# Weighted rows in a tile of their own, a precomputed count carry, and two more groups gathered as inputs, in a graph attention layer

## Chip, cores and metric

One core of a Trainium2 chip. The metric is the device time of one execution in microseconds, the median of several runs. Engines: TensorE (PE, with PEld for its weight loads), VectorE (DVE), ScalarE (ACT), GpSimd (POOL), SyncE (SP, which issues most transfers).

## What is computed

A graph attention layer with a residual: 12,500 nodes of 128 features, 200,000 edges of 64 features sorted by destination, 4 heads of 32.

```python
h = jnp.maximum(_layernorm(x, axis=-1), 0.0)
# h_src = (h @ W_node.T)[src], h_tgt the same for dst, e = edge_attr @ W_edge.T
att = jnp.sum(jnp.concatenate([h_src, h_tgt, e], axis=-1) * a, axis=-1)
att = jnp.where(att > 0, att, 0.2 * att)
m = jnp.maximum(jax.ops.segment_max(att, tgt), 0.0)
ex = jnp.exp(att - m[tgt])
denom = jax.ops.segment_sum(ex, tgt) + (num_edges - deg)[:, None] * jnp.exp(-m)
out = x + jax.ops.segment_sum((ex / denom[tgt])[:, :, None] * h_src, tgt)
```

(The last lines are shortened: segment counts are left out.)

## The kernel before

**Tiling.** The edges are cut into 392 groups of 511, each with one slot more (slot 0) for what is carried over from the group before. A group is J = 4 chunks of 128 edges on the partitions. Four groups are a quad (98 quads); two to four quads are a "super", for which one softmax is made. The destinations of a group lie within a window of WIN = 96 nodes.

**Node and index stage (L288 to L423).** For all nodes: layer norm, ReLU, product with the weights; the rows (ROW = 137 numbers: per head 32 values and a one, a count at R_CNT, four source logits from R_SRC) go to `table` in DRAM. Small index tiles (`slot`, `is_last`, `thru`, `cont`) are made beside it.

**Gathers (L128 to L139).** POOL issues one indirect DMA for each chunk of 128 edges, 16 a quad, into `ga_all`, a ring of QUADS = 8 quads. The first RAW = 4 quads gather rows of the input `x` while the table isn't there yet; they are normed and multiplied by the weights later (`normed`, L743; `converted`, L237). All others gather rows of the table. POOL works its gathers in order, each behind the last reader or writer of the ring's place that it overwrites.

**Logits (L493).** For each group DVE compares window positions with destinations (`at`, L500); PE multiplies that by the target logits (`pw`, L505) and the edge features by their weights (L508) into `lg` in PSUM. `open_logits` (L485) issues the transfers of the quad after next, its gathers included. `add_sources` (L511, called by `flush`) adds the gathered source logits on DVE (L520, L522), giving `U`.

**Softmax of a super (L533).** Transposes of `U` on PE (L548), leaky ReLU (ACT L550 and DVE L553), segmented maxima by scans on DVE (L557, L582, L584), exponentials on ACT, transposes back (`ex_ps`; `xs`; carry factors `facs`).

**Sums (L668).** For each group: DVE multiplies the gathered rows by their weights in place (L687), makes the selection matrix `hot` (L691); PE adds chunks 1 to 3 into `acc` (L696). `complete()` then finishes the group before: DVE writes the carry row (last row of the previous `acc` times a factor) into row 0 of `ga` (L634), ACT copies the count into it (L638), PE adds chunk 0 (L639), ACT copies `acc` to `pt` (L640). After a quad's last group, `divide` (L701) runs at the next `complete()`: six DVE operations, then four output transfers on SP, each with a register load (L457) for its address.

**Order.** The order is written by hand: `together` (L141) takes steps in turn from several generators, and the loop at L793 runs the sums of one quad beside the logits of a later one, with the softmax of a super beside the first sums. Each engine works its own instructions in that order.

Of the kernel before, what the change touches and what calls it, by code (L numbers as in the profile page):

```python
# [8 lines left out]
F32 = mybir.dt.float32  # L9
BF16 = mybir.dt.bfloat16  # L10
# [5 lines left out]
P = 128  # L16
# [19 lines left out]
RAW = 4  # L36
# [10 lines left out]
def kernel(  # L47
# [68 lines left out]
    thru = consts.tile([1, G], F32, name="thru")  # L116
    flag = consts.tile([1, 1], I32, name="flag")
# [4 lines left out]
    assert raw == 4 <= nq  # L122
    g_raw = sum(quads[raw - 1])

    ga_all = consts.tile([P, QUADS, QG, J, ROW], F32, name="ga")
    GA = {}

    def gather(q, rows, width):  # L128
# [3 lines left out]
        for i in range(m):  # L132
# [15 lines left out]
    with tc.manual_schedule():  # L148

        nc.sync.dma_start(srci[:, :g_raw], src_by_edge[:, :g_raw])  # L150
        for q in range(raw):
            gather(q, x, D)
# [64 lines left out]
        def gathered_inputs(q):  # L217
            return GA[q][:, :quads[q][1]].rearrange("p g j r -> p (g j) r")[:, :, 0:D]

        def raw_statistics(pool, q):  # L220
            RAWS[q] = yield from statistics(pool, gathered_inputs(q), quads[q][1] * J)

        def raw_scaled(q):

            rows = gathered_inputs(q)
            yield from scaled(rows, rows, quads[q][1] * J, *RAWS.pop(q))
# [10 lines left out]
        def converted(q, psum, turn_pool, copy):  # L237

            ga = GA[q]
            m = quads[q][1]  # L240
# [27 lines left out]
            nc.scalar.copy(rows[:, :, R_CNT], ones[:, 0:m * J])  # L268
# [19 lines left out]
        with tc.tile_pool(name="node", bufs=2) as node, tc.tile_pool(  # L288
# [10 lines left out]
            def indexed():  # L299
# [27 lines left out]
                yield  # L327

# [109 lines left out]
    with tc.tile_pool(name="work", bufs=2) as work, \  # L438
# [18 lines left out]
        def window(g):  # L457
            return nc.values_load(
                base[0:1, g:g + 1], engines=[mybir.EngineType.SP], min_val=0, max_val=N - 1,
                skip_runtime_bounds_check_because="a destination, which is a node")  # L460

        def fetch_windows(q):
# [3 lines left out]
            at = [window(g0 + i) for i in range(m)]  # L466
# [18 lines left out]
        def open_logits(q):  # L485
# [5 lines left out]
            LG[q] = ps.tile([P, QG, J, PIECES, H], F32, name="lg")  # L491
# [41 lines left out]
        def softmax(s):  # L533
# [11 lines left out]
            u = U.pop(s)  # L545
            t_ps = ps.tile([SBG * H, GE], F32, name="t_ps")
# [39 lines left out]
            ex = turned.tile([SBG * H, GE], F32, name="ex")  # L586
# [20 lines left out]
            nc.scalar.copy(facs[:, :R], fac_ps)  # L607
# [3 lines left out]
            xs = turned.tile([P, J, SBG * H], F32, name="xs", bufs=2)  # L611
            nc.scalar.copy(xs[:, :, 0:R], top_ps)
# [5 lines left out]
        begun = []  # L618
        state = {}

        def complete():

            division = state.pop("division", None)
            if begun:
                complete_group(*begun.pop())
            if division:
                divide(*division)

        def complete_group(q, i, ga, hot, pt, acc, fc):
            g0, m = quads[q]  # L630
            g = g0 + i
            if g:
                before = state["before"]
                nc.vector.tensor_tensor(  # L634
                    ga[0:1, i, 0, 0:H * HW].rearrange("p (h w) -> p h w", w=HW),
                    before[WIN:WIN + 1, 0:H * HW].rearrange("p (h w) -> p h w", w=HW),
                    fc.unsqueeze(2).to_broadcast([1, H, HW]), op=OP.mult)
                nc.scalar.copy(ga[0:1, i, 0, R_CNT:R_CNT + 1], before[WIN:WIN + 1, R_CNT:R_CNT + 1])  # L638
            nc.tensor.matmul(acc, hot[:, i, 0, :], ga[:, i, 0, :], start=False, stop=True)  # L639
            nc.scalar.copy(pt[:, i, :], acc)  # L640
            state["before"] = acc

            part = 1 if q == nq - 1 else 2 if q == nq - 2 else QG
            if (i + 1) % part == 0 or i == m - 1:
# [4 lines left out]
                state["division"] = q, pt, den, lo, i + 1  # L649
# [367 lines left out]
```

## Time and profile before

| what | value |
|---|---|
| runs | 2570.87, 2578.58, 2586.93 us; median 2578.58 us |
| profiled execution | 2600.19 us, span 2598.4 us, mean granted TensorE clock 0.536 |
| gathers | 64 of inputs (3.2 to 83.1 us), 1502 of the table (161.1 to 2473 us) |
| ACT `pt` copy L640 | 392 x 274 ns |
| DVE weighting L687 | 392 x 689 ns |
| DVE selection L691 | 384 x 545 ns |
| ACT source copy L680 | 392 x 216 ns |

In a row of the groups, the first number behind the bar is the busy time of all, the second the mean of one in ns; then comes the idle time of the engine just before them and what ended it. "Issue" is time in which the engine waited for nothing that the profile shows; "remote" is a releaser that the profile can't name. In a timeline each line gives start, duration, engine, source line and tiles, with the idle time before it in brackets. Line numbers are those of the kernel before.

### The profile page before, as it was taken

How to read it: one execution, taken by the hardware profiler on the slowest of the kernel's cores; microseconds unless marked ns; L12 is line 12 of the kernel's file. 1: busy time of each engine (PE TensorE's matmuls, PEld its weight loads, DVE VectorE, ACT ScalarE, POOL GpSimd, SP SyncE). 2: the span in 40 equal slices, each digit the busy share in tenths (PEclk: the TensorE clock that was granted, in tenths of full speed). 3: DMA queues.
4: the chain of work that ended last, by engine and by line, in shares of the span. 5: the costliest groups of instructions: out<-in, count | busy, mean ns of one | idle time of the engine just before them, and what ended most of it. 6: DMA issues, size and time to landing. Idle time of an engine off the chain costs nothing. (4 is left out here: it accounts for less than half of the span.)

```text
span 2598.4 us, 29393 instructions
## 1 busy us (share of the span) xinstructions
PE 1405.4 (54%) x7275; PEld 1256.7 (48%) x7275; DVE 1367.0 (53%) x3291; ACT 421.7 (16%) x1806; POOL 1508.0 (58%) x1609
## 2 busy tenths in 40 slices
PE   2442665555555555556555555655555555545485
PEld 1331655545545445445445544545544554444375
DVE  2441465555555545555554554654554554555486
ACT  1431411111111111111111111111111111111122
POOL 7235256666666666666666666666666666666603
PEclk9975655555555555555555555555555555555555
DMA  4342455544544454554455445454544544434430
GB/s 150 102 126 53 108 136 124 127 116 118 128 123 113 115 142 107 127 125 117 119 124 124 116 119 123 120 125 117 125 115 118 125 121 116 121 97 112 103 92 17
DMA packets 214495, 299.12 MB, mean 115 GB/s; under 512 B 86121, under 2 KB 162153, under 8 KB 204914
## 3 DMA queue, kind: packets, MB, share of 16 engines
q1 hardware_dynamic: 162512, 184.97, 26.6%
q0 software_dynamic: 50112, 109.65, 19.3%
q10 hardware_dynamic: 1698, 2.58, 0.3%
q8 instruction: 61, 1.00, 0.2%
q14 instruction: 112, 0.92, 0.1%
HBM read 270.49 MB, written 26.52 MB: 114 GB/s over the span
## 5 line engine op out<-in xcount | busy, mean ns | idle before, releaser
L137 POOL DMA_INDIRECT ga<-table,srci x1502 | 1426.7, 950 | 963.2 <-issue 406.0
L696 PE MATMUL acc<-ga,hot 128*97 128x137 f32 x2352 | 649.6, 448 | 341.3 <-ACT ga L680 225.1
L696 PEld LDWEIGHTS acc<-ga,hot 128*97 128x97 f32 x2352 | 518.2, 279 | 366.1 <-ACT ga L680 229.2
L634 DVE TENSOR_TENSOR ga<-acc,facs 1x132 f32<-1x132 f32 x391 | 115.9, 296 | 625.9 <-ACT pt L640 502.1
L639 PE MATMUL acc<-ga,hot 128*97 128x137 f32 x784 | 267.4, 444 | 289.0 <-ACT ga L638 215.5
L508 PE MATMUL lg<-wblk,ea 128*128 128x8 f32 x1568 | 410.5, 360 | 0.0
L508 PEld LDWEIGHTS lg<-wblk,ea 128*128 128x128 f32 x1568 | 383.3, 310 | 0.0
L505 PEld LDWEIGHTS <-at 96*128 96x128 bf16 x1568 | 219.7, 167 | 298.7 <-DVE at L500 115.0
L639 PEld LDWEIGHTS acc<-ga,hot 128*97 128x97 f32 x784 | 190.3, 279 | 320.3 <-ACT ga L638 235.8
L640 ACT COPY pt<-acc 97x137 f32<-97x137 f32 x392 | 107.4, 274 | 1431.8 <-remote 850.5
L505 PE MATMUL lg<-pw,at 96*128 96x12 bf16 x1568 | 170.7, 182 | 239.1 <-DVE at L500 101.2
L687 DVE TENSOR_TENSOR ga<-ga,ex_ps 128x528 f32<-128x528 f32 x392 | 270.0, 689 | 8.4 <-remote 8.0
L500 DVE TENSOR_TENSOR at<-const_ps,db 96x512 bf16<-96x512 f32 x392 | 267.1, 683 | 9.0 <-DMA db<-in_dst_dram 3.2
L691 DVE TENSOR_TENSOR hot<-const_ps,slot 128x384 f32<-128x384 f32 x384 | 209.4, 545 | 0.0
L520 DVE TENSOR_REDUCE st<-lg 128x64 f32<-128x192 f32 x98 | 35.0, 358 | 139.1 <-remote 109.7
L638 ACT COPY ga<-acc 1x1 f32<-1x1 f32 x391 | 59.9, 153 | 228.8 <-DVE ga L634 114.1
L375 PE MATMUL row_ps<-wcat,hT 128*128 128x137 f32 x198 | 40.3, 354 | 79.9 <-DVE hT L367 32.0
L600 PE MATMUL ex_ps<-ident,ex 64*128 64x64 f32 (+2 forms) x112 | 18.6, 315 | 115.6 <-ACT ex L589 49.7
L375 PEld LDWEIGHTS row_ps<-wcat,hT 128*128 128x128 f32 x198 | 34.0, 246 | 86.1 <-issue 46.0
L553 DVE TENSOR_TENSOR t_ps<-t_ps,low 64x511 f32<-64x511 f32 (+2 forms) x28 | 19.2, 687 | 104.4 <-issue 60.2
L137 POOL DMA_INDIRECT ga<-in_x_dram,srci x64 | 60.6, 947 | 20.9 <-issue 19.2
L600 PEld LDWEIGHTS ex_ps<-ident,ex 64*128 64x128 f32 (+2 forms) x112 | 13.8, 208 | 118.3 <-ACT ex L589 51.1
(131 smaller groups left out, 1131.1 us busy)
## 6 DMA issues: line engine op xcount, KB each, us to landing
db<-in_dst_dram SPq DMA_DIRECT2D x98, 768.0 KB
ea<-in_edge_t_dram SPq DMA_DIRECT2D x98, 512.0 KB
ga<-table,srci POOLq DMA_INDIRECT x1502
xw<-in_x_dram SPq DMA_DIRECT2D x392, 48.0 KB
out_dram<-res SPq DMA_DIRECT2D x392, 48.0 KB
pw<-side SPq DMA_DIRECT2D x392, 2.2 KB
table<-row SPq DMA_DIRECT2D x9, 616.5 KB
xt<-in_x_dram SPq DMA_DIRECT2D x9, 576.0 KB
```

The lines of the kernel that those rows point to most:

```text
L137: nc.gpsimd.indirect_dma_start(out=ga[:, i, j, 0:width], out_offset=None, in_=rows, in_offset=bass.IndirectOffsetOnAxis(ap=srci[:, g0 + i, ...
L375: nc.tensor.matmul(row_ps[:, t, :ROW], hT[:, t, :], wcat, start=True, stop=True)
L500: nc.vector.tensor_tensor(at[:, i, :], node_ps[0:WIN, g0 + i:g0 + i + 1].to_broadcast([WIN, GE]), db[:, i, :], op=OP.is_equal)
L505: nc.tensor.matmul(lg[:, i, j].rearrange("p k h -> p (k h)"), at[:, i, j * P:(j + 1) * P], sw, start=i + j == 0, stop=False, skip_group_ch ...
L508: nc.tensor.matmul(lg[:, i, 2 * w:2 * w + 2, 0, :], ea[:, i, w, :], wblk, start=False, stop=True, skip_group_check=True)
L634: nc.vector.tensor_tensor(ga[0:1, i, 0, 0:H * HW].rearrange("p (h w) -> p h w", w=HW), before[WIN:WIN + 1, 0:H * HW].rearrange("p (h w) -> ...
L638: nc.scalar.copy(ga[0:1, i, 0, R_CNT:R_CNT + 1], before[WIN:WIN + 1, R_CNT:R_CNT + 1])
L639: nc.tensor.matmul(acc, hot[:, i, 0, :], ga[:, i, 0, :], start=False, stop=True)
L640: nc.scalar.copy(pt[:, i, :], acc)
L687: nc.vector.tensor_tensor(val, val, heads(ex)[:, :, :, g - s0].unsqueeze(3).to_broadcast([P, J, H, HW]), op=OP.mult)
L691: nc.vector.tensor_tensor(hot[:, i, :, 0:WIN], lane_ps.unsqueeze(1).to_broadcast([P, J, WIN]), slot[:, g, :].unsqueeze(2).to_broadcast([P, ...
L696: nc.tensor.matmul(acc, hot[:, i, j, :], ga[:, i, j, :], start=j == 1, stop=False)
```

## The change

- `sums` no longer weights in place: DVE multiplies `ga` into a new tile `gw` (pairs of groups, two buffers), which PE reads. ACT fills count and source columns of `gw` once per two groups, from a constant tile `xs_all` whose ones and source columns the softmax writes.
- The count that is carried over is computed for all groups in the index stage (`came`: four products, a scan) and copied once for each super; the ACT copy L638 goes.
- The copy of `acc` to `pt` (`copied`) is issued one `complete()` later than before, the division one or two later again; three calls of `complete()` end the program.
- The leaky ReLU becomes one DVE operation on `U`, ahead of the transposes. Carry factors are copied by DVE, one row only.
- `lg` has two halves of one PSUM tile; in `all_logits` the first group's logits come before `flush`.
- SP loads four window addresses at once.
- `marks` is called quad by quad at the end, `hot` has two buffers instead of three.
- RAW stays 4, and MORE = 2 groups of quad 4 gather inputs too. They are normed beside `sums` of quad 0 and converted behind quad 3. The two other groups of quad 4 gather from the table.

```diff
@@ -33,7 +33,7 @@
 NODE_T = 9
-RAW = 4
+RAW, MORE = 4, 2
 QUADS = 8
@@ -114,22 +114,26 @@
     thru = consts.tile([1, G], F32, name="thru")
+    came = consts.tile([1, G + 1], F32, name="came")
     flag = consts.tile([1, 1], I32, name="flag")
 ...
     raw = RAW
-    assert raw == 4 <= nq
-    g_raw = sum(quads[raw - 1])
+    assert raw == 4 < nq and MORE < quads[raw][1]
+    g_raw = quads[raw][0] + MORE
+    raws = lambda q: quads[q][1] if q < raw else MORE if q == raw else 0
     ga_all = consts.tile([P, QUADS, QG, J, ROW], F32, name="ga")
-    GA = {}
-    def gather(q, rows, width):
+    GA, GATHERED = {}, set()
+    def gather(q, rows, width, lo, hi):
         g0, m = quads[q]
         ga = GA[q] = ga_all[:, q % QUADS]
-        for i in range(m):
+        for i in range(lo, hi):
             n = -(-min(E - (g0 + i) * NE + 1, GE) // P)
@@ -148,8 +152,9 @@
         nc.sync.dma_start(srci[:, :g_raw], src_by_edge[:, :g_raw])
-        for q in range(raw):
-            gather(q, x, D)
+        GATHERED.update(range(raw))
+        for q in range(raw + 1):
+            gather(q, x, D, 0, raws(q))
@@ -215,15 +220,15 @@
         def gathered_inputs(q):
-            return GA[q][:, :quads[q][1]].rearrange("p g j r -> p (g j) r")[:, :, 0:D]
+            return GA[q][:, :raws(q)].rearrange("p g j r -> p (g j) r")[:, :, 0:D]
         def raw_statistics(pool, q):
-            RAWS[q] = yield from statistics(pool, gathered_inputs(q), quads[q][1] * J)
+            RAWS[q] = yield from statistics(pool, gathered_inputs(q), raws(q) * J)
         def raw_scaled(q):
             rows = gathered_inputs(q)
-            yield from scaled(rows, rows, quads[q][1] * J, *RAWS.pop(q))
+            yield from scaled(rows, rows, raws(q) * J, *RAWS.pop(q))
         def several(n, *steps):
@@ -325,6 +329,15 @@
                 yield
+                ones_b = index.tile([P, 1], BF16, name="ones_b")
+                nc.vector.memset(ones_b, 1.0)
+                own_ps = wide_ps[0][0:1, :]
+                for j in range(J):
+                    nc.tensor.matmul(own_ps, ones_b, is_last[:, :, j], start=j == 0, stop=j == J - 1)
+                nc.vector.memset(came[:, 0:1], 0.0)
+                yield
+                nc.vector.tensor_tensor_scan(came[:, 1:G + 1], thru, own_ps, initial=0.0,
+                                             op0=OP.mult, op1=OP.add)
                 nc.vector.tensor_scalar(slot[0:1, :, 0], cont, -1.0, None, op0=OP.add)
@@ -444,8 +457,14 @@
         share_ps = const_ps[0:WIN, WIN + G:].rearrange("p (g h) -> p g h", h=H)
+        lg_all = ps.tile([P, 2, QG, J, PIECES, H], F32, name="lg")
         nc.vector.tensor_copy(lane_ps, lane)
         nc.vector.tensor_copy(node_ps, node_at)
+        xs_all = consts.tile([P, 2, J, 1 + H, SBG], F32, name="xs_all")
+        nc.vector.memset(xs_all[:, :, :, 0, :], 1.0)
         tops = consts.tile([1, H, len(supers) + 1], F32, name="tops")
@@ -454,16 +473,18 @@
             return g0, quads[q0 + m - 1][0] + quads[q0 + m - 1][1] - g0
-        def window(g):
-            return nc.values_load(
-                base[0:1, g:g + 1], engines=[mybir.EngineType.SP], min_val=0, max_val=N - 1,
-                skip_runtime_bounds_check_because="a destination, which is a node")
+        def windows(q, lo=0, hi=QG):
+            g0, m = quads[q]
+            g0, m = g0 + lo, min(hi, m) - lo
+            return nc.values_load_multi_w_load_instructions(
+                base[0:1, g0:g0 + m], engines=[mybir.EngineType.SP], min_val=0, max_val=N - 1,
+                skip_runtime_bounds_check_because="a destination, which is a node")[1]
         def fetch_windows(q):
 ...
             xw = XW[q] = work.tile([WIN, QG, D], F32, name="xw", bufs=8)
-            at = [window(g0 + i) for i in range(m)]
+            at = windows(q)
             for i in range(m):
@@ -473,8 +494,9 @@
             fetch_windows(q)
-            if q not in GA:
-                gather(q, table, ROW)
+            if q not in GATHERED:
+                GATHERED.add(q)
+                gather(q, table, ROW, raws(q), quads[q][1])
         def fetch_rows(s):
@@ -488,7 +510,7 @@
             AT[q] = work.tile([WIN, QG, GE], BF16, name="at")
-            LG[q] = ps.tile([P, QG, J, PIECES, H], F32, name="lg")
+            LG[q] = lg_all[:, q % 2]
         def logits(q, i):
@@ -543,14 +565,14 @@
             u = U.pop(s)
+            nc.vector.scalar_tensor_tensor(u[:, :, :R], u[:, :, :R], SLOPE, u[:, :, :R],
+                                           op0=OP.mult, op1=OP.max)
             t_ps = ps.tile([SBG * H, GE], F32, name="t_ps")
 ...
             low = turned.tile([P, NE], F32, name="low")
-            nc.scalar.mul(low[:R], t_ps[:R, 1:GE], SLOPE)
             yield
             att = t_ps[:R, 1:GE]
-            nc.vector.tensor_tensor(att, att, low[:R], op=OP.max)
             run = turned.tile([SBG * H, GE], F32, name="run")
@@ -604,49 +626,55 @@
             facs = turned.tile([P, SBG * H], F32, name="facs", bufs=2)
-            nc.scalar.copy(facs[:, :R], fac_ps)
+            nc.vector.tensor_copy(facs[WIN:WIN + 1, :R], fac_ps[WIN:WIN + 1, :])
             top_ps = other[:, 512 - J * SBG * H:].rearrange("p (j r) -> p j r", j=J)[:, :, 0:R]
 ...
                 nc.tensor.transpose(top_ps[:, j, :], run[:R, j * P:(j + 1) * P], ident[:R, :R])
-            xs = turned.tile([P, J, SBG * H], F32, name="xs", bufs=2)
-            nc.scalar.copy(xs[:, :, 0:R], top_ps)
+            xs = xs_all[:, s % 2]
+            nc.scalar.copy(xs[:, :, 1:, 0:m], top_ps.rearrange("p j (h g) -> p j h g", h=H))
+            nc.scalar.copy(xs[0:1, 0, 0, 0:m], came[:, g0:g0 + m])
             XS[s] = ex_ps[:, 0:J * SBG * H].rearrange("p (j r) -> p j r", j=J), xs, facs
             yield
-        begun = []
+        begun, divisions = [], []
         state = {}
         def complete():
-            division = state.pop("division", None)
+            due = [d for d in divisions if d[0] >= nq - 2 or d[-1] == 1]
+            divisions[:] = [d[:-1] + (1,) for d in divisions if d not in due]
+            full = state.pop("full", None)
             if begun:
                 complete_group(*begun.pop())
-            if division:
-                divide(*division)
-        def complete_group(q, i, ga, hot, pt, acc, fc):
-            g0, m = quads[q]
-            g = g0 + i
-            if g:
+            if full:
+                copied(*full)
+            for d in due:
+                divide(*d[:-1])
+        def complete_group(q, i, gw, hot, pt, acc, fc):
+            if quads[q][0] + i:
                 before = state["before"]
                 nc.vector.tensor_tensor(
-                    ga[0:1, i, 0, 0:H * HW].rearrange("p (h w) -> p h w", w=HW),
+                    gw[0:1, 0, 0:H * HW].rearrange("p (h w) -> p h w", w=HW),
                     before[WIN:WIN + 1, 0:H * HW].rearrange("p (h w) -> p h w", w=HW),
                     fc.unsqueeze(2).to_broadcast([1, H, HW]), op=OP.mult)
-                nc.scalar.copy(ga[0:1, i, 0, R_CNT:R_CNT + 1], before[WIN:WIN + 1, R_CNT:R_CNT + 1])
-            nc.tensor.matmul(acc, hot[:, i, 0, :], ga[:, i, 0, :], start=False, stop=True)
+            nc.tensor.matmul(acc, hot[:, i, 0, :], gw[:, 0, :], start=False, stop=True)
+            state["before"] = acc
+            state["full"] = q, i, pt, acc
+        def copied(q, i, pt, acc):
             nc.scalar.copy(pt[:, i, :], acc)
-            state["before"] = acc
             part = 1 if q == nq - 1 else 2 if q == nq - 2 else QG
-            if (i + 1) % part == 0 or i == m - 1:
+            if (i + 1) % part == 0 or i == quads[q][1] - 1:
                 lo = i - i % part
 ...
                                      AF.Exp, scale=-1.0)
-                state["division"] = q, pt, den, lo, i + 1
+                divisions.append((q, pt, den, lo, i + 1, 2))
@@ -656,7 +684,7 @@
             g0, m = quads[q]
-            hot = work.tile([P, QG, J, WIN + 1], F32, name="hot", bufs=3)
+            hot = work.tile([P, QG, J, WIN + 1], F32, name="hot")
             nc.scalar.copy(hot[:, :m, :, WIN], is_last[:, g0:g0 + m, :])
@@ -677,15 +705,21 @@
             for i in range(m):
-                nc.scalar.copy(ga[:, i, :, R_SRC:R_SRC + H], heads(xs)[:, :, :, g0 - s0 + i])
-            for i in range(m):
                 g = g0 + i
-                if q == nq - 1 - FREE and i == 1:
-                    for k in range(FREE):
-                        HOT[nq - FREE + k] = marks(nq - FREE + k)
-                val = ga[:, i, :, 0:H * HW].rearrange("p j (h w) -> p j h w", w=HW)
+                if i == 1 and nq > q + 1 >= nq - FREE:
+                    HOT[q + 1] = marks(q + 1)
+                if i % 2 == 0:
+                    gw2 = work.tile([P, 2, J, ROW], F32, name="gw")
+                    n = min(2, m - i)
+                    nc.scalar.copy(
+                        gw2[:, 0:n, :, R_CNT:R_SRC + H],
+                        xs[:, :, :, g - s0:g - s0 + n].rearrange("p j h g -> p g j h"))
+                gw = gw2[:, i % 2]
+                by_head = lambda t: t[:, :, 0:H * HW].rearrange("p j (h w) -> p j h w", w=HW)
                 nc.vector.tensor_tensor(
-                    val, val, heads(ex)[:, :, :, g - s0].unsqueeze(3).to_broadcast([P, J, H, HW]),
+                    by_head(gw), by_head(ga[:, i]),
+                    heads(ex)[:, :, :, g - s0].unsqueeze(3).to_broadcast([P, J, H, HW]),
                     op=OP.mult)
@@ -693,9 +727,9 @@
                 for j in range(1, J):
-                    nc.tensor.matmul(acc, hot[:, i, j, :], ga[:, i, j, :], start=j == 1, stop=False)
+                    nc.tensor.matmul(acc, hot[:, i, j, :], gw[:, j, :], start=j == 1, stop=False)
                 complete()
-                begun.append((q, i, ga, hot, pt, acc, fc[:, :, g - s0]))
+                begun.append((q, i, gw, hot, pt, acc, fc[:, :, g - s0]))
                 yield
@@ -720,13 +754,16 @@
             add.tensor_tensor(res[:, :n, :], res[:, :n, :], xw, op=OP.add)
+            at = windows(q, lo, hi)
             for i in range(n):
-                nc.sync.dma_start(out[bass.ds(window(quads[q][0] + lo + i), WIN), :], res[:, i, :])
+                nc.sync.dma_start(out[bass.ds(at[i], WIN), :], res[:, i, :])
         def all_logits(q):
+            open_logits(q)
+            logits(q, 0)
+            yield
             flush()
-            open_logits(q)
-            for i in range(QG):
+            for i in range(1, QG):
                 logits(q, i)
@@ -803,18 +840,20 @@
                     now, ahead = ahead[:1], ahead[1:]
-                    together(sums(q0 + k), *map(all_logits, now))
+                    together(sums(q0 + k), *map(all_logits, now), *([] if s else [normed(raw)]))
                     if s > 4:
 ...
                     complete()
+                    complete()
                     together(*late(3))
+                    together(*late(raw))
             flush()
             together(sums(nq - 1))
-            complete()
-            complete()
+            for _ in range(3):
+                complete()
             together(check_steps)
```

The parts left out bring `raws(q)` into the conversion, reuse a tile in the check of the input's order, and leave the count column of converted rows unwritten.

More of the change, by code (lines that the diff above doesn't have):

```diff
@@ L239, in converted @@
             ga = GA[q]
-            m = quads[q][1]
+            m = raws(q)
             made = []
@@ L267, in converted @@
                 ones[:, 0:1].unsqueeze(2).to_broadcast([P, m * J, H]))
-            nc.scalar.copy(rows[:, :, R_CNT], ones[:, 0:m * J])
             yield
@@ L585, in softmax @@
                                          initial=0.0, op0=OP.mult, op1=OP.max)
-            ex = turned.tile([SBG * H, GE], F32, name="ex")
+            ex = turned.tile([P, GE], F32, name="ex")
             nc.vector.memset(ex[:R, 0:1], 0.0)
@@ L764, in checked @@
             for k, (g0, n) in enumerate(blocks(G, P)):
-                rows = turned.tile([P, NE + 1], I32, name="rows")
+                rows = turned.tile([P, GE], F32, name="ex").bitcast(I32)
                 nc.scalar.dma_start(rows[:n], dst_rows[g0:g0 + n, 0:NE + 1])
-                yield
                 falls = turned.tile([P, NE], F32, name="low")
@@ L791 @@
                 together(all_logits(q), raw_statistics(raw_pool, 3))
+            assert supers[0] == (0, 2) and supers[1] == (2, 2)
             check_steps = checked()
```

## Prediction

> **What bounds the kernel now.** I read the page's busy shares first, then the slices, the table of windows, the groups by line, and last the timeline of a stretch in mid-run.
>
> ```profile
> PE 1405.4 (54%) x7275; PEld 1256.7 (48%) x7275; DVE 1367.0 (53%) x3291; ACT 421.7 (16%) x1806; POOL 1508.0 (58%) x1609
> L137 POOL DMA_INDIRECT ga<-table,srci x1502 | 1426.7, 950 | 963.2 <-issue 406.0
> L640 ACT COPY pt<-acc 97x137 f32<-97x137 f32 x392 | 107.4, 274 | 1431.8 <-remote 850.5
> L634 DVE TENSOR_TENSOR ga<-acc,facs 1x132 f32<-1x132 f32 x391 | 115.9, 296 | 625.9 <-ACT pt L640 502.1
> ```
>
> No engine is full: 54, 53 and 58%. POOL is nearest: a gather takes 0.95 us and the next starts 0.30 us later (406 us of "issue" over 1,394 gaps), 1.25 us each, 5.0 us a group of four. ACT is nearly idle, yet its `pt` copy waits 850 us for a "remote" releaser (no finished instruction accounts for it), and the carry row on DVE waits behind it for 502 us.
>
> ```profile
> 0.00:83.00 83.00, 15.54 (x55) 11.81 (x55) 14.93 (x77) 12.47 (x30) 61.50 (x72) 1.00 0.41 129
> 83.00:161.00 78.00, 45.02 (x258) 38.59 (x258) 51.44 (x224) 52.79 (x134) 0.06 (x1) 0.89 0.43 146
> 161.00:241.00 80.00, 11.39 (x44) 8.76 (x44) 6.95 (x27) 6.59 (x19) 60.40 (x64) 0.54 0.30 72
> 241.00:295.00 54.00, 36.82 (x236) 34.78 (x237) 32.08 (x95) 28.69 (x81) 0.00 (x0) 0.59 0.35 88
> ```
>
> Columns: window, length, busy us of PE, PEld, DVE, ACT, POOL, then clock, DMA share, GB/s. Where POOL gathers without a pause (0 to 83, 161 to 241) PE is busy 14 to 19% of the time; where POOL rests, 58 to 68%. From 295 to 2473 us there are 1,438 gathers, 359.5 groups, in 2,178 us: 6.06 us a group (5.97 between 1000 and 1500), against 5.0 of POOL and about 3.2 each of PE and DVE (54%, 53% of 6). The timeline shows why:
>
> ```profile
> 1484.94 0.66 PE L639 MATMUL acc<-ga,hot 128*97 128x137 f32 x2
> ...
> 1486.45 0.22 PE L505 MATMUL lg<-pw,at 96*128 96x12 bf16 x2 [0.85 <-issue]
> ...
> 1488.82 0.94 POOL L137 DMA_INDIRECT ga<-table,srci  x1 [0.30 <-issue]
> ...
> 1491.72 0.28 ACT L640 COPY pt<-acc 97x137 f32<-97x137 f32 x1 [8.21 <-remote]
> 1491.95 0.94 POOL L137 DMA_INDIRECT ga<-table,srci  x1 [2.19 <-remote]
> 1492.02 0.30 DVE L634 TENSOR_TENSOR ga<-acc,facs 1x132 f32<-1x132 f32 x1 [4.55 <-ACT pt L640]
> ...
> 1492.96 0.69 DVE L687 TENSOR_TENSOR ga<-ga,ex_ps 128x528 f32<-128x528 f32 x1
> ```
>
> L639 ended at 1485.60, but ACT, which waits for it, started at 1491.72: 1.96 us after POOL's last gather ended (1489.76). POOL itself waits for the same L639, to overwrite that group's rows. So while POOL gathers, the others learn late that PE is done. I counted pauses (a gather with over 1 us of idle before it) from 400 to 2300 us: 137 runs of 8 or 12 gathers mostly (58 and 59; also 19 of 4, one of 16), on average 2.31 groups, with pauses of 2.57 us. PE completions in the first 5 to 5.5 us of a run are seen promptly, later ones nearly all about 2.2 us after it stops. The loop: POOL runs c groups, stops at a row not yet known to be free, all is seen 2.2 us later, everybody works from then until about 5.5 us into the next run. Check: 5.0 + (2.57 − 0.30)/2.31 = 5.98 us a group, as measured.
>
> Here a rule could undo the reading. The Trainium skill (Perfetto Trace Analysis, "Tensor Engine Instruction") says that a PE end is an estimate, not an observation. By the rule the 6 us after L639 could be PE still at work, then shortening the chain behind PE is worth nothing (time unchanged, 2,579 us). The rows decide otherwise: PE, which works in order, started L505 at 1486.45, so L639 was past by then. I use the rows.
>
> **The change, part by part**, against the profiled execution (2,600.19 us, span 2,598.4).
>
> *The ring's release.* DVE now writes weighted rows into `gw`, so POOL's gather waits for DVE's multiply instead of L639; the built program has 370 POOL waits on DVE (11 before), 77 on PE (365 before). In group number, rows are free about three groups earlier, since the multiply of group n+3 is issued about when L639(n) is seen. That offset is won once: about 3 groups go from a 6 us pace into a tail without gathers, where the pace is near 4; I take −7 us. But the multiply of n+3 stands in DVE's order behind the carry row of n+1, which waits for the last matmul of n. So at each stop POOL still needs PE's completion to be seen, and after it DVE's carry row (0.30), often a logits compare or `add_sources` (0.6), and the multiply (0.69): 1.5 to 2 us more. Before, POOL restarted at once at that point, and the multiply came later: after the restart at 1491.95 it ended at 1493.65. Bounds for the pause: 2.57 (multiply already done) to 5.0 (a divide, 2.2 us, lies ahead of it too); taken 4.05.
> *What the longer pause gives back.* The working stretch is pause − 2.2 + 5.5: before 5.87 us for 2.31 groups, 2.54 us a group; after 7.35 us. The cost of a group in it falls: L634 no longer waits on L640 (0.24 us at 1483.02), L638 (153 ns ×391) goes, L553 (687 ns ×28, 0.05 a group): to 2.29. So c = 7.35/2.29 = 3.2, and a group takes 5.0 + (4.05 − 0.30)/3.2 = 6.17 us against 5.98, **+0.19 ×355 = +67 us**. By the ends: a pause of 2.57 with 2.29 gives c 2.56 and 5.89 (−33 us); 5.0 with 2.54 gives c 3.27 and 6.44 (+161 us).
> *ACT and semaphores.* L638 and four 216 ns copies a quad become one copy per two groups; `pt` copies lag one group. ACT is 16% busy, so its 60 us lie beside all else; only the hops counted above stand on the path. PE updates fall from 2256 to 1416. If late delivery depended on their number it would ease; in the 80 us run one got through in about 10 us (L263 at 175.30 and 185.11), however few there were, so 0; else the onset moves from 5.5 to at most 7.5 us: c = 4.1, 5.92 us, −23 us.
> *SP.* 785 register loads become 201. SP issues for two quads ahead; four `pw` issues stretched over 12.6 us (at 182.97) and no group waited for them (L500 waits 3.2 us in all, for `db`). 0; if that cover were gone, 0.7 us a quad, 70 us at most.
> *Leaky-relu before the transposes.* L550 (588 ns, waits 159.5 us for remote) and L553 go; one DVE operation 128x256 comes, 0.44 us by a line through 128x64 (269) and 64x511 (677): on DVE −7 us in all, already in 2.29. The skill (SBUF, "Who interferes with whom") says that a DVE instruction with two SBUF inputs contends with a GpSimd instruction that reads SBUF; the new one has two. By the rule 28 × 0.44 = up to 12 us are lost by gathers. The nearest row is L722, two SBUF inputs: at 1485.09 it took 0.71 us beside a gather of 0.94 us, both as usual. I take 0.
> *Double logits, deferred divide, spread marks.* The first logits go ahead of the flush, the divide behind a later carry row: an order change on DVE with the same instruction count. Where the divide falls in a pause it costs its 2.2 us, in one of four groups; that is in the pause's bound.
> *Two more raw groups.* Eight gathers move ahead of the table: the first run ends at 93 instead of 83, so the backlog and the table come about 10 us later (171), and the second run is 56 instead of 64 gathers, 10 us shorter. Net 0. If the node stage does use the 10 us it is −4. The conversion costs eight transposes, eight products, four copies of 0.39, two of 0.69, and norms beside `sums(0)`, on a path where the engines wait for each other: +7 us (0 to +12). The `came` row is some five small operations in the index stage, beside POOL's pause, +1.
>
> Sum: +67 − 7 + 7 + 1 = +68: 2,668 for a profiled execution. That of before is 21.6 us above the median of the runs, so about **2,647 us**.
>
> **Rivals.**
> - *About the same.* Four groups in each cycle: 5.0 + 3.75/4 = 5.94 us; −15 us with nothing else, 2,565 to 2,600. For it: 12-gather runs are already half of all. Against: DVE is full in the working stretches (1492.0 to 1497), so 1.84 us a group is needed.
> - *Faster.* POOL's row is freed by DVE, whose signals are prompt, and the lead of three groups covers the late PE signal. For it: DVE and ACT signals show no delay. If the multiply does not have to wait for PE (two `gw` pairs would have to suffice for c groups), pauses shrink to below 1.6 us per 3 groups: 5.43, −195 us, 2,385. A half success, 5.7, gives 2,480. Against: `gw` itself is freed by PE. It decides once the pause divided by c falls below 0.9 us.
> - *Much slower.* Divide or the softmax's chain stands ahead of the multiply in most pauses: 6.44 and beyond, 2,740 to 2,790. For it: 2.2 us every quad and some 12 us of DVE every 16 groups. Against: DVE takes part of it while PE's signals are held back.
> - *Nothing.* Ring and hops cost nothing because pauses are set by SP or DMA (share 0.5): 2,579. Against: POOL's waits end at L639 of the same group.
>
> **How the numbers follow.** Forecast (1 to 4.5% slower) 0.45, much slower 0.20, same or nothing 0.15, faster 0.20. Within 1% is what the measurement cannot tell from no change (the three runs lie 0.6% apart). So faster 0.20, same 0.15, slower 0.65. The forecast's own range is 2,605 to 2,695. For 8 in 10 I take in half of each flank: 2,520 to 2,770.
>
> **What would show it.** Right: POOL's gathers wait for the multiply; fewer pauses (about 115 instead of 137 in 1,900 us), each 3.7 to 4.5 us, runs of 12 and 16; late PE signals as before; 6.1 to 6.3 us a group in the middle; the second run of gathers still ends near 241. Wrong: pauses under 3 us with runs of 12 or more, or PE's signals prompt in long runs (then faster); pauses at 5 us and more, with the divide in them (then much slower).

## The result and the profile after

The changed kernel takes 2,832.31 us (median of four, 2,828.62 to 2,835.44) against 2,575.08 us, **1.099 times** the time before (95% interval 1.0949 to 1.1032). The forecast was slower, 2,647 us, with 2,770 us as the upper end: right in sign, with 2.7% where 9.9% came. The profiled execution took 2,833.38 us, its span is 2,831.5 us. The kernel before took 2,568 to 2,611 us in some groups of runs, this result's among them, and 2,026 to 2,036 us in others, with the same program, so every ratio is taken against the runs of before beside it.

The busy shares and the groups of the page, changed kernel:

```profile
PE 1427.4 (50%) x7303; PEld 1248.0 (44%) x7303; DVE 1374.0 (49%) x3337; ACT 333.2 (12%) x1205; POOL 1504.5 (53%) x1609
L141 POOL DMA_INDIRECT ga<-table,srci x1494 | 1415.4, 947 | 1176.0 <-DVE gw L720 559.8
L660 DVE TENSOR_TENSOR gw<-acc,facs 1x132 f32<-1x132 f32 x391 | 115.8, 296 | 926.6 <-remote 817.0
```

Hardly any engine has more work: POOL 1,504.5 us (1,508.0 before), DVE 1,374 (1,367), PE 1,427 (1,405); ACT has 88 us less. All are idle longer. POOL's idle before gathers grew from 963 to 1,176 us, and its largest part now names DVE's multiply (L720). The carry row (L660) waits for an unnamed releaser for 817 us, as ACT's copy did before for 850 us.

The windows of the same kernel (columns as in the table of windows shown before):

```profile
0.00:83.00 83.00, 15.53 (x55) 11.81 (x55) 14.87 (x78) 13.95 (x33) 61.55 (x72) 1.00 0.40 129
...
171.00:241.00 70.00, 11.94 (x44) 9.46 (x44) 8.22 (x29) 9.83 (x26) 51.20 (x55) 0.53 0.27 73
...
1000.00:1500.00 500.00, 249.83 (x1290) 217.64 (x1290) 241.66 (x551) 41.45 (x174) 281.91 (x297) 0.51 0.44 110
```

The last of these stretches in the kernel before:

```profile
1000.00:1500.00 500.00, 281.98 (x1444) 253.06 (x1444) 268.80 (x607) 66.68 (x329) 317.54 (x335) 0.50 0.50 120
```

In the middle 297 gathers fall into 500 us where 335 did: 6.7 us a group instead of 6.0. The second run of gathers goes from 173.3 to 243.1, some 2 us later than worked out (171 to 241).

Where the 233 us of span went can be read from the start of the multiply of a given group in both traces: group 32 starts 36 us later (532.1 against 496.1); from there to group 360 it takes 2,160.6 us instead of 1,970.0, which is **191 us**; behind it 6.4 us are lost.

The runs and pauses of POOL, counted in the traces as for the prediction (400 to 2300 us, a pause being over 1 us of idle before a gather):

| kernel | pauses | groups a run | mean pause, us | DVE busy in a pause, us | us a group |
|---|---|---|---|---|---|
| before | 137 | 2.31 | 2.57 | 0.48 | 6.00 |
| changed | 77 | 3.74 | 6.31 | 3.33 | 6.62 |

5.0 + (6.31 − 0.30)/3.74 gives 6.61, so the same sum holds with other terms. The same pauses, sorted by what DVE did inside them:

| inside the pause (over 0.3 us of it) | changed: pauses, mean us | before: pauses, mean us |
|---|---|---|
| softmax | 34, 8.33 | 32, 2.72 |
| a division, no softmax | 3, 7.30 | none |
| neither | 40, 4.51 | 105, 2.52 |

So it is the softmax that makes the long pauses of the changed kernel, while before it cost POOL next to nothing. A pause of 8 to 12 us comes at nearly every 64th gather of the changed kernel, once a super of four quads. One of them in the timeline of the changed kernel:

```profile
1479.75 0.95 POOL L141 DMA_INDIRECT ga<-table,srci  x1 [0.31 <-issue]
...
1483.20 0.15 DVE L602 COPY col<-ex_ps 64x1 f32<-64x1 f32 x1 [5.22 <-remote]
1483.45 1.28 DVE L604 TENSOR_TENSOR_SCAN t_ps<-kp,col,t_ps 64x511 f32<-64x511 f32 x1
...
1486.72 0.63 ACT L611 ACTIVATE ex<-ex 64x511 f32<-64x511 f32 x1 [11.46 <-DVE ex L610]
...
1489.15 0.23 DVE L629 COPY facs<-acc 1x64 f32<-1x64 f32 x1 [0.78 <-PE acc L627]
1489.41 0.70 DVE L720 TENSOR_TENSOR gw<-ga,ex_ps 128x528 f32<-128x528 f32 x1
...
1490.38 0.95 POOL L141 DMA_INDIRECT ga<-table,srci  x1 [9.69 <-DVE gw L720]
```

POOL stopped at 1480.70 (1479.75 + 0.95), after 16 gathers. PE's signal was seen 2.5 us later (1483.20). Then the rest of the softmax ran, because the multiply that frees POOL's row uses its exponentials and stands behind it on DVE: POOL rested 9.69 us. Before, the row was freed by L639 of an earlier group, and POOL went on at about 2.2 us while softmaxes and divisions ran beside its next gathers.

### The profile page after: what moved, and what is told of

Same layout as the page of the kernel before. It is cut to its first block, busy times and chain, and to the rows that moved or that the text cites. A ratio compares the mean times of both kernels' runs of the same rounds, so it can differ in the third digit from the quotient of the medians.

```text
span 2831.5 us, 27061 instructions
## 1 busy us (share of the span) xinstructions
PE 1427.4 (50%) x7303; PEld 1248.0 (44%) x7303; DVE 1374.0 (49%) x3337; ACT 333.2 (12%) x1205; POOL 1504.5 (53%) x1609
## 4 chain that ended last, share of the span: by engine, by line
another core or an unknown queue 36%; DVE 33%; PE 15%; issue 6%; DMA 1%; ACT 1%; SPq 0%; DVEq 0%; POOL 0%; POOLq 0%; ACTq 0%
PE acc L730 6%; DVE gw L720 6%; DVE at L522 6%; DVE hot L725 4%; PE lg L530 3%; DVE gw L660 3%; PE acc L664 2%; DVE res L756 2%; DVE res L752 2%; DVE t_ps L604 1%; DVE t_ps L606 1%; PE acc L266 1%; PE acc L627 1%; DVE U L544 1%
## 5 line engine op out<-in xcount | busy, mean ns | idle before, releaser
L730 PE MATMUL acc<-gw,hot 128*97 128x137 f32 x2352 | 642.5, 444 | 67.9 <-DVE hot L725 16.7
L664 PE MATMUL acc<-gw,hot 128*97 128x137 f32 x784 | 267.6, 444 | 667.7 <-DVE gw L660 579.2
L660 DVE TENSOR_TENSOR gw<-acc,facs 1x132 f32<-1x132 f32 x391 | 115.8, 296 | 926.6 <-remote 817.0
L730 PEld LDWEIGHTS acc<-gw,hot 128*97 128x97 f32 x2352 | 514.1, 277 | 99.6 <-issue 55.2
L664 PEld LDWEIGHTS acc<-gw,hot 128*97 128x97 f32 x784 | 185.4, 274 | 707.2 <-DVE gw L660 609.2
L527 PEld LDWEIGHTS <-at 96*128 96x128 bf16 x1568 | 212.6, 165 | 284.3 <-issue 138.4
L720 DVE TENSOR_TENSOR gw<-ga,ex_ps 128x528 f32<-128x528 f32 x392 | 270.7, 690 | 1.3
L141 POOL DMA_INDIRECT ga<-in_x_dram,srci x72 | 68.3, 949 | 23.3 <-issue 21.6
L692 POOL TENSOR_SCALAR hot<-lane,slot 128x96 f32<-128x96 f32 x32 | 17.1, 554 | 105.2 <-ACT hot L688 94.1
L752 DVE TENSOR_TENSOR res<-pt,const_ps 96x512 f32<-96x512 f32 (+2 forms) x102 | 67.5, 662 | 7.1 <-DMA out_dram<-res 3.1
```

The source lines that it names most:

```text
L141: nc.gpsimd.indirect_dma_start(out=ga[:, i, j, 0:width], out_offset=None, in_=rows, in_offset=bass.IndirectOffsetOnAxis(ap=srci[:, g0 + i, ...
L527: nc.tensor.matmul(lg[:, i, j].rearrange("p k h -> p (k h)"), at[:, i, j * P:(j + 1) * P], sw, start=i + j == 0, stop=False, skip_group_ch ...
L660: nc.vector.tensor_tensor(gw[0:1, 0, 0:H * HW].rearrange("p (h w) -> p h w", w=HW), before[WIN:WIN + 1, 0:H * HW].rearrange("p (h w) -> p ...
L664: nc.tensor.matmul(acc, hot[:, i, 0, :], gw[:, 0, :], start=False, stop=True)
L720: nc.vector.tensor_tensor(by_head(gw), by_head(ga[:, i]), heads(ex)[:, :, :, g - s0].unsqueeze(3).to_broadcast([P, J, H, HW]), op=OP.mult)
L730: nc.tensor.matmul(acc, hot[:, i, j, :], gw[:, j, :], start=j == 1, stop=False)
```

## The experiments

**Theory.** PE's signals are seen late while POOL gathers. With the ring freed by DVE's multiply, POOL runs on longer, more is late when it stops, and in the pause it also waits for DVE's chain. **Rivals:** the tile itself (its two buffers, DVE's writes); the order (deferred copies and divisions, logits ahead of the flush); the two raw groups.

Not every run shows PE's signals late. In the changed kernel's trace above 104 of 287 carry rows (400 to 2300 us) start over 1 us after the modelled end of the product that they wait for, with DVE idle; in another trace of the same program, below, none of 338 does (from 400 us on). I call the first kind of run "late" and the second "prompt". The loss is seen in late runs alone, so these decide.

### Rows weighted in place: first, second and third time

```diff
-                    gw2 = work.tile([P, 2, J, ROW], F32, name="gw")
+                    gw2 = ga[:, i:i + 2]
```

> The changed kernel with the rows weighted in place again, so that a gather waits for PE's last matmul as before; everything else of the change stays. Theory (the ring's release behind DVE's multiply makes POOL's runs and pauses long): back near the kernel before, 2,540 to 2,610 us, runs of about 2.3 groups with pauses of about 2.6 us. Rival 'order' (deferred copies and divisions, logits ahead of the flush): stays within 2,780 to 2,850 us. Rival 'raw groups': stays too.

> The changed kernel with rows weighted in place, as in the first experiments. Where the kernel before takes 2,029 us: 2,039 us again. Where it takes about 2,575 us: theory 2,540 to 2,610 us, pauses near 2.6 us; rivals 'order' and 'raw groups' 2,780 to 2,850 us.

> The changed kernel with rows weighted in place, a third time, since the chips so far were of two kinds: on two of them the kernel before takes 2,029 us and PE's signals are prompt, on the others 2,575 to 2,600 us with late signals. With late signals: theory 2,530 to 2,640 us, runs of 2 to 2.7 groups, pauses of 2.4 to 3.2 us; rivals 'order' and 'raw groups' 2,780 to 2,860 us. With prompt signals 2,030 to 2,045 us, as before.

The first two met prompt signals: 2,039.31 us, 1.0047 times before (1.0030 to 1.0064), and 2,038.17, 1.0044 (1.0030 to 1.0058). They tell nothing of the loss. The third met late ones: 2,636.98 against 2,577.76 us, **1.023** (1.0183 to 1.0281; two runs). Its page:

```profile
L141 POOL DMA_INDIRECT ga<-table,srci x1494 | 1415.0, 947 | 1001.0 <-issue 472.9
```

POOL's idle is 1,001 us, where it was 1,176 in the changed kernel and 963 before. The time is as expected; the mean pause of 3.33 us and the runs of 2.87 groups are somewhat longer than expected (up to 3.2 us and 2.7 groups), at 6.08 us a group. The rivals "order" and "raw groups" needed 2,780 us or more: they fall as causes of the bulk.

### The tile kept, the ring freed by PE: twice

```diff
+            nc.tensor.matmul(bank[0:1, 256:320], rows[:, 0:1], rows[:, 0:64], start=True, stop=True)
```

(behind the last matmul of a group; `rows` are the unweighted rows of its first chunk, `bank` the PSUM bank of `acc`. The gathers of the other three chunks stand behind the first one on POOL.)

> The changed kernel, tile and all, with one small product more per group (1 row of 64, from the unweighted rows, result unused), put behind the group's last matmul: POOL's gather then waits for PE again although rows are weighted in a tile of their own. Theory: 2,540 to 2,620 us, pauses near 2.6 us. Rival 'the tile itself' (its two buffers make DVE wait for PE, or DVE's writes are dearer): stays at 2,780 to 2,860 us.

> The changed kernel, tile, deferred copies and all, with the small product from the unweighted rows behind each group's last matmul, so that POOL's gather waits for PE again. So far it met prompt signals only (2,043 us beside 2,029). With late signals: theory (the release of the ring through DVE makes the loss) 2,590 to 2,690 us, near the 2,637 us of in-place weighting; rival 'the tile itself': 2,780 to 2,860 us. With prompt signals 2,035 to 2,050 us.

First prompt: 2,042.81 us, 1.0066 (1.0049 to 1.0083). Then late: 2,639.80 against 2,570.94 us, **1.026** (1.0212 to 1.0313; two runs). The groups of this late run:

```profile
L141 POOL DMA_INDIRECT ga<-table,srci x1494 | 1412.7, 946 | 995.4 <-issue 407.9 <-remote 170.3 <-PE acc L665 127.7
...
L665 PE MATMUL acc<-ga 128*1 128x64 f32 x784 | 143.6, 284 | 0.0
L660 DVE TENSOR_TENSOR gw<-acc,facs 1x132 f32<-1x132 f32 x391 | 115.9, 296 | 631.5 <-remote 388.8 <-PE acc L732 130.8 <-PE acc L665 48.3
```

POOL waits for PE again and its idle is back from 1,176 to 995 us. PE has 144 us of products more, and still the kernel stands at 1.026 times before, where the changed one stood at 1.099. Pauses are 3.03 us, DVE is busy for 0.90 us of them (3.33 in the changed kernel), 6.06 us a group. Softmax falls into 7 of its 120 pauses (34 of 77 in the changed kernel). Tile, deferred copies, order and raw groups are all still there, so freeing the ring by DVE without PE is what costs some 7 of the 10 points. With the in-place run, which undoes it in another way and lands within 0.3 points, this is the decisive experiment.

### The changed kernel as it is, beside before

> The changed kernel as it is, beside the kernel before, because in the first experiments the kernel before itself took 2,029 us, POOL gathered without a pause and no signal of PE was late. Where the kernel before takes about 2,029 us again: theory says no cost of the change, 2,025 to 2,045 us, because its loss needs late signals. Where the kernel before takes about 2,575 us: 2,820 to 2,840 us again. Rival 'the loss is the change's own work or order': 8 to 10% slower in both cases.

2,035.84 us, **1.0022** (1.0011 to 1.0034), prompt, as expected for that case. The windows of this run:

```profile
0.00:83.00 83.00, 52.23 (x275) 43.40 (x276) 60.62 (x283) 55.39 (x139) 61.55 (x72) 0.87 0.71 231
...
1000.00:1500.00 500.00, 332.78 (x1731) 302.53 (x1731) 320.58 (x729) 55.74 (x238) 378.52 (x399) 0.50 0.62 143
```

POOL does the same 61.55 us of gathers in the first 83 us, but PE is busy for 52 us beside them instead of 15.5. In the middle POOL gathers without a pause, 399 in 500 us, 5.0 us a group. A stretch of its timeline:

```profile
1003.49 0.67 PE L664 MATMUL acc<-gw,hot 128*97 128x137 f32 x2
...
1003.91 0.94 POOL L141 DMA_INDIRECT ga<-table,srci  x1 [0.30 <-issue]
...
1004.19 0.30 DVE L660 TENSOR_TENSOR gw<-acc,facs 1x132 f32<-1x132 f32 x1 [0.45 <-PE acc L664]
```

The carry row starts 0.03 us after PE's modelled end, in the middle of a POOL run. Without late signals the change costs 0.2%: its own work and order make no loss of 10% by themselves.

### Without the two raw groups

```diff
-RAW, MORE = 4, 2
+RAW, MORE = 4, 0
```

(and without their norm and conversion)

> The changed kernel without the two raw groups of the fifth quad. Theory: within 15 us of the changed kernel (2,820 to 2,845 us), the pace in the middle the same 6.6 us a group. Rival 'raw groups': under 2,780 us.

2,035.12 us in one run, prompt, beside 2,029.41 of before and 2,035.84 of the changed kernel in the runs above: the raw groups move nothing that one run shows. The expected 2,820 to 2,845 us were for late signals, with which this was not tried.

### The tile alone on the kernel before

```diff
-                val = ga[:, i, :, 0:H * HW].rearrange("p j (h w) -> p j h w", w=HW)
+                if i % 2 == 0:
+                    gw2 = work.tile([P, 2, J, ROW], F32, name="gw")
...
+                gw = gw2[:, i % 2]
```

(and two `hot` buffers instead of three, to make room, with `marks` called quad by quad at the end)

> The kernel before with only the tile of weighted rows added (pairs of groups, two buffers; its source and count columns copied by ACT), and two hot buffers instead of three to make room. Theory: about as slow as the changed kernel, 2,760 to 2,880 us, with runs of 3.5 groups or more and pauses of 5 to 7 us. Rivals 'order' and 'raw groups': near 2,580 us.

> The kernel before with only the tile of weighted rows added, again, for a chip with late signals (on a chip with prompt signals it took 2,037 us beside 2,029). With late signals: theory 2,740 to 2,860 us, 3.3 groups a run or more, pauses over 5 us, since in-place weighting took 7 of the 10 per cent of the change away. Rival 'the tile does harm only together with the deferred copies and divisions': 2,560 to 2,640 us. With prompt signals 2,030 to 2,045 us.

> The kernel before with only the tile of weighted rows added, a third time, still for a chip with late signals, where it hasn't run. With late signals: theory 2,740 to 2,860 us, 3.3 groups a run or more, pauses over 5 us. Rival 'the tile does harm only together with the deferred copies and divisions': 2,560 to 2,640 us. With prompt signals 2,030 to 2,045 us.

> The kernel before with only the tile of weighted rows added, a fourth time: it hasn't run yet where signals are late. With late signals: theory 2,740 to 2,860 us, 3.3 groups a run or more, pauses over 5 us. Rival 'the tile does harm only together with the deferred copies and divisions': 2,560 to 2,640 us. With prompt signals 2,030 to 2,045 us.

> The kernel before with only the tile of weighted rows added, a fifth time, since it hasn't run yet where signals are late. With late signals: theory 2,740 to 2,860 us, 3.3 groups a run or more, pauses over 5 us. Rival 'the tile does harm only together with the deferred copies and divisions': 2,560 to 2,640 us. With prompt signals 2,030 to 2,045 us.

> The kernel before with only the tile of weighted rows added, beside the paced one. With late signals: theory 2,740 to 2,860 us, 3.3 groups a run or more, pauses over 5 us. Rival 'the tile does harm only together with the deferred copies and divisions': 2,560 to 2,640 us. With prompt signals 2,030 to 2,045 us.

> The kernel before with only the tile of weighted rows added, some time after the others. With late signals: theory 2,740 to 2,860 us, 3.3 groups a run or more, pauses over 5 us. Rival 'the tile does harm only together with the deferred copies and divisions': 2,560 to 2,640 us. With prompt signals 2,030 to 2,045 us.

All seven met prompt signals: 2,035.74 to 2,040.33 us, 1.0035 to 1.0044 times before. So where signals are prompt the tile costs about 0.4%. The expected 2,740 to 2,880 us were for late signals: whether the tile alone, without deferred copies and divisions, brings the whole loss there stays open.

### Half of the table's gathers left out, both kernels

```diff
-            for j in range(n):
+            for j in range(n if rows is x else 2):
```

(and the ring set to zero at the start; the sums leave out half of the edges)

> The kernel before with half of the table's gathers left out (two of four chunks of each group; the others keep zeros or old rows, so the sums are not the reference's) and the ring zeroed once at the start. POOL then needs 2.5 us a group. Theory: where PE's signals are prompt, POOL is the bound at 5.0 us a group, so this falls to what PE (1,380 us busy) and DVE (1,370 us) allow, 1,500 to 1,700 us. Where they are late: 1,700 to 2,300 us. Rival 'the bound is the chain of sums, not POOL': over 1,900 us with prompt signals.

> The changed kernel with the same half of the gathers left out. It shows what the shorter chains (no count copy, later pt copies, one leaky-relu operation) are worth when POOL doesn't hide them. Theory: 2 to 8% less than the kernel before with half of the gathers where signals are prompt. Rival 'the change's order is dearer in itself': as long or longer.

Both late (the full kernel before beside them: 2,599.11 us): 1,825.32 us, within the 1,700 to 2,300 expected, and 1,924.28 us. With half of the gathers in the kernel before, the `pt` copy's waits now name PE, and one of 2.4 us is left without a name:

```profile
POOL ga L137 <- PE acc L640: 576.5, 259, 11.4
ACT pt L641 <- PE acc L640: 517.1, 293, 4.3
```

(In this kernel lines are one further on: L641 is the `pt` copy.) POOL's runs there are mostly 2 or 4 gathers, so they end within the first 5 us, in which the prediction found signals prompt. With the same gathers left out the changed kernel takes 5.4% longer. The 2 to 8% less were expected of prompt signals, so they were not tested; "as long or longer", the rival, is what came, but the release through DVE is in this run too, and its longest pauses are the longer ones again (95th percentile 8.7 us against 6.0). What the shorter chains are worth when POOL is not the bound isn't known.

### Short breaks in POOL's runs

```diff
+                    nc.gpsimd.tensor_scalar(pace, lane, part[:, 0:1], None, op0=OP.is_equal)
```

(ahead of every four table gathers, on the kernel before)

> The kernel before with one small operation (a comparison over 128 by 96, 0.55 us by the row of such operations on POOL) ahead of every four table gathers on POOL, so that POOL never issues more than four gathers in a row. With half of the gathers, in runs of two with pauses between, no signal of PE was late. With late signals in the kernel before: theory, if a break of some 0.6 us lets the signals through, 2,430 to 2,520 us, no pause over 2 us in the middle, 5.6 us a group; if a break that short doesn't, about 392 breaks of 0.6 us more, 2,600 to 2,830 us. With prompt signals: POOL is the bound, so +0.55 to 0.65 us x 376 groups, 2,230 to 2,280 us.

> The kernel before with one small POOL operation ahead of every four table gathers, again, since it has run only where signals are prompt (2,233 us beside 2,030, 0.54 us for each of 376 operations). With late signals: theory, if a break of some 0.6 us lets the signals through, 2,430 to 2,520 us and no pause over 2 us; if it doesn't, 2,600 to 2,830 us. With prompt signals 2,225 to 2,240 us.

Both prompt: 2,233.27 us, 1.1005 (1.0973 to 1.1037), and 2,231.96. That is 203.6 us for 376 operations of 545 ns, 0.54 us each: with prompt signals POOL is the bound, microsecond for microsecond (205.0 us of added work). Whether breaks help with late signals stays open.

## Why the prediction was wrong, by its own steps

- **What bounds the kernel now: right for the runs it was made from.** The loop of run, stop, flush and working stretch holds in all late runs with the full gathers. (A detail: the 1,394 gaps of "issue" sum to 425 us with the gathers of inputs, not 406; 0.30 us each is right.)
- **"The ring's release" is the step that failed, in the size of the pause.** The wait on DVE, behind the carry row and PE's signal, came as described. The pause was taken as 4.05 us, with 5.0 as the worst; it measured 6.31, and a quarter of the pauses are over 7.50. Of the 3.74 us added, 2.85 are DVE's work inside the pause (3.33 against 0.48). The term that was missing is the softmax. Pauses without softmax or division took 4.51 us, within the 4.1 to 4.6 that the prediction's own 2.57 and 1.5 to 2 us give; 34 of the 77 had softmax work of DVE in them and took 8.33 us. They come to 34 × 3.82 = 130 us more in the 1,900 us counted, an estimate, near the 153 us (220 − 67) by which the forecast of this step fell short. The bound was also too low by its own terms: with a divide of 2.2 us on top they give 6.3 to 6.8 us, not 5.0. Divisions alone mattered little, since three pauses hold one (7.30 us). The "much slower" rival named the softmax, but was priced at the same pause of 5.0 us.
- **The flush was taken as fixed at 2.2 us.** It grows with the run: in the kernel before a `pt` copy that waited for late signals started 1.86 us (median) after the end of a run of 8 gathers and 2.52 us after one of 12; in the changed kernel the carry row started 2.95 us after runs of 16 and 3.62 us after runs of 20. So longer runs pay more at their end, which goes with the other 0.9 us.
- **"What the longer pause gives back": too little to pay for it.** Runs of 3.2 groups were forecast, 3.74 came. The cost of a group in the working stretch isn't told by the sum: with a flush of 2.2 us it is (6.31 − 2.2 + 5.5)/3.74 = 2.57 us, against 2.54 before; with the 2.95 us measured it is 2.37, near the 2.29 assumed. With 6.31 and 3.74 in their places the step gives 6.61 us a group, where 4.05 and 3.2 gave 6.17. Times the 355 groups of the forecast that is some 220 us instead of 67.
- **ACT and semaphores at 0: nothing speaks against it.** ACT has 88 us less work and PE 37% fewer updates, and signals were late as often as before: 104 of 287 carry rows over 1 us late, where it was 118 of 316 `pt` copies.
- **Leaky-relu: right in size.** 392 ns on average (425 at full width; 440 forecast). The loss of up to 12 us by the rule of the Trainium skill (SBUF — State Buffer, "Who interferes with whom") that a DVE instruction with two SBUF inputs contends with a GpSimd instruction that reads SBUF could hardly arise here: 2 of the 28 operations ran beside a gather, and those two gathers took 1.17 us (the mean is 0.95). In the prompt run of the same program 25 of them did, and the gathers beside them took 951 ns on average, the others 949: there it doesn't show.
- **Two raw groups: the window nearly right, the cost not told apart.** The second run of gathers ends at 243, where it ended at 241 before. By group 32 the changed kernel is 36 us behind; the two late kernels that free the ring by PE are 11 and 8.5 us behind there, near the 8 us forecast for conversion and count row. The rest of the 36 us goes with the release.
- **The tail of −7 us didn't come:** 6.4 us lost instead.
- **The rivals:** "about the same" came near in its runs (four groups; 3.74 measured), not in its pause. "Faster" rested on DVE's prompt signals. What made the multiply depend on PE is the order on DVE: it follows straight on the operation ahead of it (1.3 us of idle before it in all 392), so the release of `gw` by PE, named as the reason against, did not hold it. Its case without late signals exists, at 5.0 us a group, but for both kernels, and then the change gains nothing, since POOL's 1,566 gathers at 1.25 us are 1,958 of some 2,030 us.
- **The remaining 2.3 to 2.6%** with the release undone (59 and 69 us in the medians; in the traces about 40 us of span, the profiled execution of before being longer than the median: 8.5 to 11 in the head, 20 to 26 in the middle, 5 to 11 in the tail) come from the rest of the change, among it deferred divisions and logits ahead of the flush, or in one of the two from the added product. Which of them wasn't tried.

## What to carry to other kernels

When a wait is moved from one engine to another, list everything that stands ahead of the new releaser on its engine, the rarest and longest chain included, and bound the wait with that chain, not with the usual step. Freeing a buffer earlier for a producer that isn't the bound can let it run until it disturbs the consumers, and pay it back with a longer stop. Where an engine's waits have no named releaser, compare only with runs of the kernel before taken beside it: here their cause came and went.

## What was not expected of the hardware

That PE's signals come late at all, and that with the same program they are late or prompt, was not expected. Late signals go with 27% more time (2,575.08 against 2,029.41 us), with the same granted clock (mean 0.536 and 0.538 in the two profiled runs with late signals above; 0.533 to 0.542 in prompt runs of the variants) and the same gathers (944 to 947 ns median). Late runs differ from prompt ones in two things in the trace. PE's completions reach the others late while POOL gathers: the carry row L660 waited up to 14.1 us for its unnamed releaser. And SP's plain register moves take 132 ns on average instead of 29, with a median of 29 in both, so a part of them takes long, up to 1.4 us (read from the two traces of the changed kernel). DVE's and ACT's operations are as long as before. The gathers' data itself isn't late: by the DMA packets of the late runs of both kernels it landed 1.2 to 1.4 us (median) after the end of its issue, at the start of a run and at its 20th gather alike. It doesn't go with the chip: two chip numbers showed late and prompt signals both (2,577.76 and 2,032.45 us of the kernel before under one, 2,599.11 and 2,029.87 under the other), against the two kinds of chip that one expectation above supposed. What sets the one or the other, no run here shows.
